# Two graph layers on one core: block turns on VectorE and an exchange through DRAM in place of TensorE transposes

## The chip, the cores and the metric

The kernel runs on one core of one Trainium2 chip. Each of the core's engines has its own queue of instructions: TensorE (PE; its weight loads are listed as PEld), VectorE (DVE), ScalarE (ACT), GpSimd (POOL) and SyncE (SP), which here only issues DMAs. POOL issues DMAs too. The metric is device time in microseconds (us), the median of several runs. Durations of instructions come from one further execution, which the hardware profiler recorded.

## The reference

There are 16 graphs (batches) of 1024 nodes with 128 features, and an adjacency matrix of zeros and ones for each. Two residual blocks follow one another.

```python
h = relu(layernorm(x))                       # block 0
for i in range(4):                           # gated layers, GRU cell
    m = einsum('bjn,bjd->bnd', adj, h @ weight[i])
    r = sigmoid(xr + hr); z = sigmoid(xz + hz); n = tanh(xn + r * hn)
    h = (1 - z) * n + z * h                  # xr, xz, xn from m @ w_ih[i].T, hr, hz, hn from h @ w_hh[i].T
x = x + h * nodemask[:, :, None]
h = relu(layernorm(x))                       # block 1
for i in range(4):                           # graph convolution
    h = relu(einsum('bnm,bmc->bnc', adj, h @ W[i]) + b[i])
    h = gamma[i] * (h - mean) * rsqrt(var + 1e-5) + beta[i]   # mean and var over all batches and nodes
x = x + h
```

## The kernel before

`exact_path` does the work. (A flag, found by looking at the low bits of every adjacency value, would choose the slower `general_path` for other data; it isn't taken here.) All values are f32; a matmul with the adjacency takes the features as the sum of two f32r tiles, a rounded part and a rest (`hw[0]` and `hw[1]`, 128 nodes by 128 features for each block), so that the sum is as good as f32.

**The first stage** (to about 1240 us) is block 0. The weight of a layer is folded into the input weights of the gates (`w_mT`), so h itself is aggregated. The gates want h with the features on the partitions (128 x 1024, two halves of 512 nodes), the aggregation wants it as weights with the nodes on the partitions. So h is turned in each layer: `features_times` with `w` None (L491) makes eight 128x128 transposes on TensorE (L498), ScalarE copies the rounded part out of PSUM (L502), VectorE subtracts the rest (L503). `turn` (L639, L647) brings the normalized y of a new batch into the layout of the gates; `tail_norm` (L651, L657) turns the last h back, adds it to x with the mask (L660), takes the sums of the next layer norm, and stores the result (`xmid_d`, and its normalized form, `ymid_d`).

Two streams, A for the even batches (`sa`) and B for the odd ones (`sb`), take turns. `half_step(one, two)` (L856) does the gates of `two` (`gate_step`, L781, once for each half: twelve f32 matmuls in pairs, sigmoid, two VectorE operations, tanh, sigmoid, three VectorE operations) and the aggregation of `one` (`agg_step`, 32 matmuls of 128x512, L525, then ScalarE copies of the result m, L770, that the next half-step's gates take). Before them it splits `one`'s h (L859). A layer of both streams is two half-steps, a pair of batches eight. Beside this run:

- `finish` (L829): when a batch has gone through its four layers, `tail_norm`, and `take` (L736), which loads the eight row tiles of 512 KB of the stream's next batch (`load_rows`, L577, on SP) into the slots of the old ones. A stream aggregates a new batch's layer 0 in the half-step that follows.
- `copy_rows` (L572): the next adjacency is copied from the input into a DRAM scratch (`raw`), 8 DMAs of 512 KB on POOL; the loads take it from there.
- `transpose_rows` (L591): GpSimd casts a row tile to bf16, SP issues a DMA transpose into `adjT`, which POOL stores (`adjT_d`, 2 MB) for the second stage. One tile `adjT` serves both streams, two tiles `half1` hold the casts.
- `ahead` (L817): loads x of the next batch (POOL), normalizes it, turns it. `look_on` (L838): four `look`s (L589) at a time, a maximum over the low bits of a row tile on VectorE.

In the start-up (L880) the order of all engines is that of the code. In the steady loop (L995 to L1004) this holds for POOL and SP alone; on PE, DVE and ACT a planner orders what is ready by its own costs, with a few edges by `behind` (L683). POOL and SP work strictly in order: an instruction that waits holds up everything behind it.

**The second stage** is block 1: the stored turned adjacency is loaded (`load_adjT`, L1018), widened to f32r, and aggregated; the last part adds x and stores the output.

Of the kernel before, what the change touches and what calls it, by code (L numbers as in the profile page):

```python
# [8 lines left out]
F32 = mybir.dt.float32  # L9
# [332 lines left out]
def exact_path(  # L342
# [57 lines left out]

    def hw_tiles(b, name):
        return [keep.tile([P, N], F32R, tag=f"hw{b % 2}{s}", name=f"{name}_{s}") for s in range(2)]
# [14 lines left out]
    maskT = const.tile([P, B * NB], F32, tag="maskT", name="maskT")  # L417
    NV = 2 * 3 * L + 3 * L
# [27 lines left out]
    def turn_small(vn, mn):  # L446
# [6 lines left out]
        nc.vector.tensor_copy(maskT, pt[:, : B * NB])  # L453

# [79 lines left out]
    with ExitStack() as st:  # L534
# [3 lines left out]
        def load_x(b, eng):  # L538
            xt = flat(f"x{b}")
            eng.dma_start(xt, x[b].rearrange("(k p) c -> p k c", p=P))  # L540
            return xt

        raws = {}
# [28 lines left out]
        def copy_rows(b):  # L572
            raws[b] = rawd.tile([N, N], F32, tag="raw", name=f"raw{b}")
            for j in range(NB):
                nc.gpsimd.dma_start(raws[b][j * P : (j + 1) * P, :], adj[b][j * P : (j + 1) * P, :])
# [15 lines left out]
        def transpose_rows(b, row, j, adjT):  # L591

            t = work.tile([P, N], BF16, tag="half1", name=f"half{b}_{j}", bufs=2)
            nc.gpsimd.tensor_copy(t, row.bitcast(F32))  # L594
            nc.sync.dma_start_transpose(adjT[:, :, j * P : (j + 1) * P], t)

        def norm(xt, y, name):

            norm_apply(xt, y, norm_stats(xt, name))
# [39 lines left out]
        def turn(y, name, hT=None, func=AF.Copy):  # L639

            if hT is None:
                hT = work.tile([P, N], F32, tag="h", name=f"h_{name}", bufs=7)
# [8 lines left out]
        def tail_norm(b, xt, hT):  # L651

            for hf in range(NH):
                pt = tmp(f"pt_x{b}_{hf}")
                for q in range(BH):
                    k = hf * BH + q
                    nc.tensor.transpose(pt[:, q * P : (q + 1) * P], hT[:, k * P : (k + 1) * P], ident)  # L657
                for q in range(BH):
                    k = hf * BH + q
                    nc.vector.scalar_tensor_tensor(  # L660
                        xt[:, k, :],
                        pt[:, q * P : (q + 1) * P],
                        maskT[:, b * NB + k : b * NB + k + 1],
                        xt[:, k, :],
                        ALU.mult,
                        ALU.add,
                    )
# [5 lines left out]
            nc.gpsimd.dma_start(xmid_d[b].rearrange("(k p) c -> p k c", p=P), xt)  # L673

            def rest():
                norm_apply(xt, y, nt)
# [4 lines left out]
        written = [True]  # L681

        def behind(*inss):  # L683

            es = ExitStack()
            for ins in () if written[0] else inss:
                es.enter_context(tc.issue_after(ins.ins))
            return es

        class Stream:  # L690


            def __init__(self, first):
                self.b, self.i, self.rest, self.tag = first, 0, None, "AB"[first % 2]
                self.opened = None
# [31 lines left out]
            def prepare(self, b, xt):  # L727
                y = work.tile([P, N], F32, tag=f"y{self.tag}", name=f"y_in{b}", bufs=1)
                norm(xt, y, f"in{b}")
                self.ready = b, xt, y  # L730

            def prepare_turn(self):
                b, xt, y = self.ready
                self.ready = xt, y, turn(y, f"in{b}")
# [6 lines left out]
            def split_step(self):  # L741
                nm = f"{self.b}_{self.i}"
                self.hw = hw_tiles(self.b, f"ghw{nm}")
                for g in range(NH):
                    if self.i > 0:
                        features_times(None, self.hT, self.hw, g, f"g{nm}")
                        continue
                    self.split_high(g)
                    self.split_low(g)

# [30 lines left out]
            def gate_step(self, hf, between=None):  # L781
# [30 lines left out]
                self.last_dve = nc.vector.tensor_add(ho, ho, r)  # L812
                if hf == NH - 1:
                    self.hT = self.new
                    self.i += 1

            def ahead(self):  # L817

# [477 lines left out]
```

## Time and profile before

| | |
|---|---|
| median of 3 runs | 1840.94 us (1840.56 to 1841.36) |
| the profiled execution | 1840.61 us, of which the span from its first to its last instruction is 1838.8 us |
| busy, share of the span | PE 99%, PEld 68%, DVE 67%, ACT 56%, POOL 15% |
| granted TensorE clock | 0.999 |
| DMA | 381 MB, mean 207 GB/s |
| row loads, `row<-raw` | 112 of 512 KB, 5.8 us from issue to landing in the median |
| copies of the adjacency, `raw<-in_adj_dram` | 112 of 512 KB, 11.6 us |

Busy times count an instruction from its start to its end, and matmuls overlap; so durations of PE are read from the distance of starts. A table of instructions in time gives start, duration, engine, line, operation, output and inputs, and in brackets how long the engine was idle before and what ended that.

### The profile page before, as it was taken

The page shows a single profiled execution, that of the slowest core. Times are in us where ns is not written, and L with a number is a line of the kernel's source. Part 1 is how long each engine was busy: PE and PEld are TensorE (multiplying, and loading weights), DVE is VectorE, ACT ScalarE, POOL GpSimd, SP SyncE. Part 2 cuts the span into 40 slices and gives each one's busy share as a digit, 9 for nine tenths or more (in the row PEclk, how much of TensorE's full clock was granted, in tenths as well). Part 3 has the DMA queues.
Part 4 walks back from the last instruction along what each step waited for, and adds up shares of the span by engine and source line. Part 5 has one row for each costly group of instructions (what it writes and reads, how often), then busy time and mean ns, then how long its engine had stood idle before and what let it go on. Part 6 is the DMA issues. An engine that isn't in the chain of part 4 may idle for free.

```text
span 1838.8 us, 21960 instructions
## 1 busy us (share of the span) xinstructions
PE 1821.5 (99%) x7326; PEld 1254.2 (68%) x7326; DVE 1225.6 (67%) x2244; ACT 1035.8 (56%) x1577; POOL 285.0 (15%) x378
## 2 busy tenths in 40 slices
PE   9999999999999999999999999999999999999997
PEld 6566666656566666666565666667778888888886
DVE  7656667567666766766766757676666666666665
ACT  5544454553545554445355353467777767767764
POOL 4131320230231042023023013011100000000011
PEclk9999999999999999999999999999999999999999
DMA  7189775575486386567557546349876676767676
GB/s 264 39 247 317 209 229 195 162 206 192 159 233 180 126 233 178 196 172 217 218 159 206 178 145 172 103 159 332 291 248 228 212 256 204 257 209 260 210 249 242
DMA packets 256280, 381.21 MB, mean 207 GB/s; under 512 B 149932, under 2 KB 155856, under 8 KB 252320
## 3 DMA queue, kind: packets, MB, share of 16 engines
q1 hardware_dynamic: 237968, 245.95, 44.2%
q0 software_dynamic: 17664, 133.53, 20.4%
q8 instruction: 59, 0.97, 0.2%
q14 instruction: 61, 0.50, 0.1%
q10 hardware_dynamic: 528, 0.26, 0.0%
HBM read 287.39 MB, written 117.44 MB: 220 GB/s over the span
## 4 chain that ended last, share of the span: by engine, by line
PE 94%; DVE 2%; ACT 2%; issue 1%; DMA 1%; SPq 0%; POOL 0%; DVEq 0%; ACTq 0%; POOLq 0%
PE pm L525 24%; PE pc_m L525 12%; PE g_r L790 11%; PE g_z L790 11%; PE pc_g_r L525 6%; PE pc_g_z L525 6%; PE g_hn L790 6%; PE g_xn L790 6%; PE hw_c L500 4%; PE hw_g L498 2%; PE pw_g_hn L1096 1%; PE pw_g_xn L1096 1%; PE pt_in L647 1%; PE pt_x L657 1%; PE pc_g_r L510 1%
## 5 line engine op out<-in xcount | busy, mean ns | idle before, releaser
L525 PE MATMUL pm<-row,ghw 128*128 128x512 f32 x2048 | 515.6, 406 | 0.1
L525 PEld LDWEIGHTS pm<-row,ghw 128*128 128x128 f32 x2048 | 383.2, 188 | 112.6 <-issue 36.9
L525 PE MATMUL pc_m<-wide,chw 128*128 128x512 f32 x1024 | 246.0, 395 | 0.0
L525 PEld LDWEIGHTS pc_m<-wide,chw 128*128 128x128 f32 x1024 | 190.5, 188 | 42.3 <-issue 4.3
L807 ACT ACTIVATE r<-r,vecs 128x512 f32<-128x512 f32 x128 | 92.3, 721 | 216.8 <-DVE r L804 216.8
L525 PE MATMUL pc_g_r<-wide,chw 128*128 128x512 f32 x464 | 187.0, 403 | 0.3 <-ACT chw L502 0.3
L525 PE MATMUL pc_g_z<-wide,chw 128*128 128x512 f32 x464 | 180.9, 390 | 0.0
L594 POOL CAST half<-row 128x1024 bf16<-128x1024 f32 x128 | 139.7, 1108 | 250.9 <-DMA adjT<-half 169.6
L1028 DVE CAST wide<-packed 128x1024 fp32r<-128x1024 bf16 x160 | 110.0, 692 | 74.5 <-PE pc_m L525 56.4
L1028 DVE CAST wide<-block 128x1024 fp32r<-128x1024 bf16 x160 | 110.2, 691 | 73.2 <-PE pc_g_z L525 40.2
L503 DVE TENSOR_TENSOR ghw<-hw_g,ghw 128x512 fp32r<-128x512 f32 x96 | 62.0, 686 | 129.7 <-ACT ghw L502 129.5
L1026 ACT CAST wide<-block 128x1024 fp32r<-128x1024 bf16 x96 | 100.6, 1048 | 59.3 <-PE pc_m L525 34.3
L803 DVE SCALAR_TENSOR_TENSOR r<-g_hn,vecs,r 128x512 f32<-128x512 f32 x128 | 95.4, 745 | 56.8 <-ACT r L802 31.3
L1026 ACT CAST wide<-packed 128x1024 fp32r<-128x1024 bf16 x96 | 100.7, 1049 | 55.6 <-PE pc_g_z L525 23.7
L790 PE MATMUL g_r<-m,w_mT 128*128 128x512 f32 x256 | 130.7, 592 | 0.0
L790 PE MATMUL g_z<-m,w_mT 128*128 128x512 f32 x256 | 130.7, 592 | 0.0
L790 PE MATMUL g_xn<-m,w_mT 128*128 128x512 f32 x256 | 130.7, 592 | 0.0
L589 DVE TENSOR_REDUCE low<-row 128x1 f32<-128x1024 uint16 x112 | 128.6, 1210 | 0.0
L808 ACT ACTIVATE z<-g_z,brz 128x512 f32<-128x512 f32 x128 | 87.1, 680 | 71.0 <-PE g_z L790 71.0
L770 ACT COPY m<-pm 128x512 f32<-128x512 f32 x128 | 68.8, 586 | 101.3 <-PE pm L525 101.2
L802 ACT ACTIVATE r<-g_r,brz 128x512 f32<-128x512 f32 x128 | 87.7, 685 | 60.3 <-PE g_r L790 59.5
L810 DVE TENSOR_TENSOR h<-h,r 128x512 f32<-128x512 f32 x96 | 74.6, 777 | 62.4 <-ACT r L807 62.4
(176 smaller groups left out, 2764.0 us busy)
## 6 DMA issues: line engine op xcount, KB each, us to landing
packed<-adjT_d SPq DMA_DIRECT2D x256, 256.0 KB, 5.9
block<-adjT_d SPq DMA_DIRECT2D x256, 256.0 KB, 5.4
raw<-in_adj_dram POOLq DMA_DIRECT2D x112, 512.0 KB, 11.6
row<-raw SPq DMA_DIRECT2D x112, 512.0 KB, 5.8
adjT_d<-adjT POOLq DMA_DIRECT2D x16, 2048.0 KB, 7.9
xmid_d<-x POOLq DMA_DIRECT2D x16, 512.0 KB, 4.8
y<-ymid_d POOLq DMA_DIRECT2D x16, 512.0 KB, 5.1
ymid_d<-y_mid POOLq DMA_DIRECT2D x15, 512.0 KB, 3.0
```

The costliest lines, as they stand in the source:

```text
L500: nc.tensor.matmul(pt[:, q * P : (q + 1) * P], src, w, start=True, stop=True)
L525: nc.tensor.matmul(pm[hf], hw[s][:, j * P : (j + 1) * P], rows[j][:, hf * HALF : (hf + 1) * HALF], start=(j == 0 and s == 0), stop=(j == N ...
L589: nc.vector.tensor_reduce(low[:, k : k + 1], lows, axis=AX.X, op=ALU.max)
L594: nc.gpsimd.tensor_copy(t, row.bitcast(F32))
L790: nc.tensor.matmul(po, wT[:, i, g * C : (g + 1) * C], rhs, start=start, stop=stop)
L802: nc.scalar.activation(r, pr, AF.Sigmoid, bias=brz[:, 3 * i : 3 * i + 1])
L803: nc.vector.scalar_tensor_tensor(r, phn, b_hn(i), r, ALU.add, ALU.mult)
L807: nc.scalar.activation(r, r, AF.Tanh, bias=b_in(i))
L808: self.last_act = nc.scalar.activation(z, pz, AF.Sigmoid, bias=brz[:, 3 * i + 1 : 3 * i + 2])
L810: nc.vector.tensor_sub(ho, hin, r)
L1026: nc.scalar.copy(r, t)
L1028: nc.vector.tensor_copy(r, t)
```

## The change

Batches 0 and 1 (`plain`) are done as before. For the others the transposes of h and y no longer run on TensorE. VectorE turns a half (128 x 512) in blocks of 32x32, which leaves each block in the right orientation and in the wrong group of 32 partitions. The half is then written to a DRAM scratch (`cross`, 256 KB) and read back by four DMAs, one for each group of 32 partitions, which pick its blocks from all four groups. All these DMAs are issued on SP.

```diff
+        def exchange_out(t, name):
+            d = rawd.tile([P, HALF], F32, tag="cross", name=f"cross_{name}", bufs=6)
+            nc.sync.dma_start(d, t)
+            return d
+
+        def exchange_in(d, t):
+            src = d.rearrange("(t r) (s x) -> s r t x", t=4, s=4)
+            for s in range(4):
+                nc.sync.dma_start(t[s * 32 : (s + 1) * 32, :].rearrange("r (t x) -> r t x", t=4), src[s])
...
+        def turn_across(y, name):
+            hT = work.tile([P, N], F32, tag="h", name=f"h_{name}", bufs=7)
+            for hf in range(NH):
+                cols = slice(hf * HALF, (hf + 1) * HALF)
+                t = half_tile(f"ty_{name}_{hf}").bitcast(F32)
+                nc.vector.transpose(t, y[:, cols].rearrange("p (k a c) -> p a k c", a=4, c=32))
+                exchange_in(exchange_out(t, f"{name}_{hf}"), hT[:, cols])
+            return hT
```

The gates end with the turn and the way out, and the way back follows: the first half's at once, the second half's (`two.exchange()`) in `half_step`. In the next half-step, between the gates' operations of the other stream, ScalarE and VectorE split the returned tile (`split_part`), which they read in runs of 32 columns.

```diff
             def gate_step(self, hf, between=None):
...
+                else:
+                    nc.vector.tensor_add(ho, ho, r)
+                    if not plain(self.b):
+                        t = half_tile(f"th{nm}").bitcast(F32)
+                        nc.vector.transpose(t, ho)
+                        self.outs[hf] = exchange_out(t, f"h{nm}")
+                if hf == 0:
+                    self.exchange()
...
+        def turn_rows():
+            for b, row, j in waiting_rows[:2]:
+                if j == 0:
+                    adjTs[b] = turned_tile(f"adjT{b}")
+                transpose_rows(b, row, j, adjTs[b])
+                if j == NB - 1:
+                    nc.gpsimd.dma_start(adjT_d[b], adjTs[b])
+            del waiting_rows[:2]
+            for dst, src in copies[:2]:
+                nc.gpsimd.dma_start(dst, src)
+            del copies[:2]
+
+        def beside_aggregation(one, two):
+            if one.b + 2 < B and one.i == 2:
+                one.next_apply()
+            if two.ends:
+                two.ends.pop(0)()
+            if one.ends:
+                one.ends.pop(0)()
+            if two.b + 2 < B and two.i == 2:
+                two.next_sums()
+            if one.b + 2 < B and one.i == 3:
+                one.next_turn()
+            one.look_on()
+
         def half_step(one, two, gated=None, halfway=None):
-            if one.i > 0:
+            if one.i == 1:
+                one.give_rows()
+            by_turns = plain(one.b) and one.i > 0
+            if by_turns:
                 one.split_step()
-            two.gate_step(0)
-            two.gate_step(1)
+            for hf in range(NH):
+                two.gate_step(hf, None if by_turns else lambda: one.split_part(hf))
             if gated:
                 gated()
-            if one.i == 0:
-                one.split_step()
+            turn_rows()
+            two.exchange()
+            if two.i == 1:
+                two.ahead()
+            turn_rows()
+            beside_aggregation(one, two)
             one.agg_step(0)
             if halfway:
                 halfway()
-            if one.rest:
-                with behind(two.last_act):
-                    one.rest()
-                one.rest = None
-            two.ahead()
-            one.look_on(two)
             one.agg_step(1)
             two.finish()
```

`next_sums`, `next_apply` and `next_turn` are the former normalization and turn of the next batch's y, the last now with `turn_across` in layer 3. `tail_norm` of the batches 2 to 13 reads the exchanged tile in place of a turn on TensorE, one half-step later than before; the batches 14 and 15 keep their last turn on TensorE. The copies of the adjacency and its row transposes, eight of each at once before, come as two and two in each half-step.

The block turns put the nodes of a half in another order (node 128q+32k+i at place 128k+32q+i). So for these batches x and the adjacency's rows are copied to DRAM in that order (`order_x`, and the two patterns in `copy_rows`), the cast of a row tile reorders its columns, the mask has a second map (`maskB`), `xmid` is brought back by a DRAM copy, and the ReLU of the last convolution writes its columns in the reference's order.

The steady loop's order is that of the code on every engine:

```diff
-        with tc.manual_schedule(engines={mybir.EngineType.Pool, mybir.EngineType.SP}):
-            written[0] = False
+            turn_mask(load_mask())
+        with tc.manual_schedule(engines=every):
             for s in range(2, B // 2 * L):
                 half_step(sa, sb)
                 half_step(sb, sa)
```

In the second stage two kinds of buffers change places (`load_adjT`, `fetch_x`).

## The prediction

> **What bounds the kernel now.** I read the busy shares first, then the chain, then PE's, VectorE's and SP's instructions in time over one pair of batches (563.5 to 713.5 us), then the table of stretches. The page:
>
> ```profile
> PE 1821.5 (99%) x7326; PEld 1254.2 (68%) x7326; DVE 1225.6 (67%) x2244; ACT 1035.8 (56%) x1577; POOL 285.0 (15%) x378
> ...
> PE 94%; DVE 2%; ACT 2%; issue 1%; DMA 1%; SPq 0%; POOL 0%; DVEq 0%; ACTq 0%; POOLq 0%
> ```
>
> TensorE is busy all the time and the chain is TensorE's. PE in time, one half-step (gates of one stream, aggregation of the other) and what surrounds it:
>
> ```profile
> 589.97 1.04 PE L498 MATMUL hw_g<-ident,h 128*128 128x128 f32 x8
> 590.84 1.02 PE L790 MATMUL g_r<-h,w_hhT 128*128 128x512 f32 x2
> ...
> 595.99 1.02 PE L790 MATMUL g_r<-h,w_hhT 128*128 128x512 f32 x2
> ...
> 600.74 7.85 PE L525 MATMUL pm<-row,ghw 128*128 128x512 f32 x32
> 608.42 1.03 PE L657 MATMUL pt_x<-ident,h 128*128 128x128 f32 x8
> 609.29 1.02 PE L790 MATMUL g_r<-h,w_hhT 128*128 128x512 f32 x2
> ```
>
> Read the starts, since matmuls overlap: eight turns take 590.84-589.97 = 0.87 us, one half of the gates 595.99-590.84 = 5.15, so both 10.30, and the aggregation 608.42-590.84-10.30 = 7.28. A half-step is 18.45 us, with no gap. Eight of them and two more groups of eight turns (L647) make 149.3, and the stretch says:
>
> ```profile
> 563.50:713.50 150.00, 150.00 (x530) 92.64 (x529) 102.69 (x202) 74.66 (x128) 31.32 (x41) 1.00 0.61 190
> ```
>
> Columns: stretch, then PE, PEld, DVE, ACT, POOL, granted clock, share of the 16 DMA engines, GB/s. What leaves PE here is time won, until another thing is late. The second stage (from about 1240 us) keeps its work.
>
> **What goes.** For each batch from 2 on: turns of h in layers 1 to 3 (3 x 8), of y (8), and for batches 2 to 13 of the last h (8). That is 14 x 4 + 12 = 68 groups of eight, 68 x 0.87 = **59 us**: 52 in the six pairs 2/3 to 12/13, 5 in the last pair, 2 in the first. A half-step of a middle pair becomes 17.58.
>
> **What VectorE and ScalarE get.** Neither the 32x32 turn nor a strided read of a turned tile is in this trace. The nearest row for the turn is a 128x512 f32 operation on VectorE:
>
> ```profile
> 593.69 0.75 DVE L803 SCALAR_TENSOR_TENSOR r<-g_hn,vecs,r 128x512 f32<-128x512 f32 x1
> ...
> 597.70 0.69 DVE L812 TENSOR_TENSOR h<-h,r 128x512 f32<-128x512 f32 x1
> 598.84 0.75 DVE L803 SCALAR_TENSOR_TENSOR r<-g_hn,vecs,r 128x512 f32<-128x512 f32 x1 [0.45 <-PE g_hn L790]
> ```
>
> I take 0.69; the bounds are 0.26 (a 128x128 pass, L609) and 1.21 (the 128x1024 16-bit pass, L589). The turned h lies 597.70+0.72+0.69-590.84 = 8.3 us into the half-step for the first half. The second half starts behind it and is turned at 13.7 (4.0 from its first operation to its last add, 0.72, 0.69). The split's subtraction (0.69) fits the 0.79 in which VectorE waited for the tanh, and ScalarE's copy (0.6) fits its 1.8 us wait for VectorE. Beside the aggregation come at most 4.7 (four looks of 1.21 pipelined, or multiply-adds and sums, 609.48 to 614.4) and two more turns (1.3). So VectorE ends at 18.4 to 19.7, and is wanted again at 17.58+2.85 = 20.4. It fits with 1 us to spare. At 1.21 per turn it would be over by about 1 us in some half-steps: +0 to 15 in all. ScalarE: root, table load and eight ReLUs follow VectorE's second half and end at 17.6 as the m copies become due. I put 0; at 0.3 each time it is 8.
>
> **What SP's queue gets; here I see the loss.** Each exchange is one issue out, a wait until it has landed, and four issues in; all stand on SP in written order, in front of whatever comes later, the row loads of the stream's next batch included. Issue is 0.32 us (L581). SP's stores of 128 and 256 KB landed in 2.1 at best (L1243; medians of 2.4 to 4.7 in its groups); I take 2.3. One exchange holds SP for 2.3+0.1+4x0.32 = **3.7 us**; bounds 3.3 and 4.4. Half-step (B, layer 3) has four in a row: two of A's last h, two of B's next y. SP starts the second at 13.7, so it is free at 13.7+3x3.7 = 24.8, which is 7.2 us into the next half-step. Only then come A's eight row loads. Now they come early:
>
> ```profile
> 582.90 7.58 SPq L581 DMA_DIRECT2D row<-raw  x8
> ```
>
> That is 17.8 us before the aggregation of 600.74 uses them. Afterwards PE wants the first row 10.3 us in, one more each 0.91, and is done at 17.58. The first lands 3.2 after its issue at best (L581), the others 1.55 apart (512 KB at the 339 GB/s of 603 to 613):
>
> ```profile
> 603.00:613.00 10.00, 10.00 (x42) 7.02 (x41) 9.18 (x25) 2.79 (x5) 0.92 (x1) 1.00 0.96 339
> ```
>
> Row 7 lands at 7.2+3.2+7x1.55 = 21.3, and its four matmuls end at 22.3: **PE waits 5 us** (3.4 and 7.4 at the bounds). Next, B's last two exchanges are queued behind these loads: out at 22.8, SP through with both at 22.8+1.3+3.7 = 27.8, B's loads start 5.4 into the following half-step of which they are wanted 10.3 in; row 7 lands at 19.5: **3 us** more (2 to 5). Then A's exchanged h of that half-step waits behind B's loads, comes some 4 us late to the split, and moves tanh, the z that frees a bank, and the m copies: **2 us** (0 to 5). So 10 us at a change of batch.
>
> How often? The change from the first pair has no exchange of h (batches 0 and 1 are turned on TensorE): two exchanges end 3.4 us into the half-step and cost nothing. The six later ones cost 6 x 10 = **60 us** (35 to 100).
>
> **DMA and POOL in the middle half-steps.** Today's share is 0.61 of 150 = 92 us a pair. Twenty exchanges of 2 x 256 KB and 2 MB of reordered x and xmid are 12.6 MB, 37 us at 339 GB/s; together 129 of about 141. The row turns of one stream wait on SP for the other's adjT store (7.9 to landing) in front of an exchange; its half arrives 1 to 2 us late, most of it absorbed (PE wants the split only 14 us in). I put 1.5 a pair, 9 in all (0 to 30). The mask's turn, two maps of x and the reordered copies are small or long before use: 0 (0 to 8). Stage two's strided ReLU: 0; covered by aggregation.
>
> The Trainium skill, "DMA: Bandwidth & Descriptors", rules for kernel authors, speaks against splitting: transfers to disjoint partitions share the same engines, one 128-partition transfer is better, and under 64 KB one mostly pays overhead; the four parts of each return are 64 KB. The same page's fit, about 2.0 us + bytes / 436 GB/s, gives an estimate of 2.6 us for the store where the trace has 2.1 at best; by 2.6 an exchange holds SP 4.0 us and the row wait is about 1 us longer per change of batch.
>
> **Sum.** The profiled execution took 1840.61 us (span 1838.8 and 1.8 around it); the median of the runs is 1840.94, so the two can be read as one. 1840.6 - 59 + 60 + 9 = **1850**. The signs depend on sizes that nearly cancel, and I say so.
>
> **Rivals.**
> - *The loads arrive in time* (faster). If SP is through earlier, because stores to DRAM land faster than 2.1 us for a lone transfer or the loads of 4 MB find idle engines, the waits shrink to about 2 us a pair: 1840.6 - 59 + 12 = 1794. For it: PE wants rows one after another, and between 573 and 583 the DMA share is 0.19. Against it: every issue-to-landing in the trace is above 2 us, and four lie in a row. It decides if a boundary costs under 9 us.
> - *DMA becomes the bound* (slower). A 512 KB store in 512-byte pieces (xmid, 4.8 us) lands 1.8 us later than one in 4 KB pieces (ymid, 3.0). If the returns cost 0.9 each by that, 20 x 0.9 = 18 us come on top of 129: 147 of DMA in a pair of 141, unevenly spread (raw copies landed in 11.6). Six pairs of 147 + 10 instead of 150 are +42, less 7 in the others: about 1876; with VectorE's lateness 1890. For it: today's share already reaches 1.05 in places. Against: most of the load is not urgent.
> - *Written order itself costs* where the planner filled gaps: some 15 us on top of the forecast, 1865; or the turns are only replaced without effect on the cadence, no change.
>
> **Chances.** Forecast (boundary waits of 6 to 15 us) 0.50: 0.07 of it faster, 0.09 the same, 0.34 slower. Loads in time 0.27, faster. DMA bound 0.20, slower. The last 0.03: 0.01 faster, 0.02 slower. A measurement of this kernel can tell about 0.2% (3.7 us) from no change. Faster 0.35, same 0.09, slower 0.56. For the range I take 1790 (most of the case of loads in time) to 1895 (most of the DMA case); the likeliest case alone is 1825 to 1880.
>
> **What would show it.** Right: no L498, pt_in or pt_x groups for later batches; PE steps of 17.6 us inside a pair; PE idle in front of L525 released by a DMA of row<-raw, at each change of batch from batch 2 on, with the row loads issued only some 7 us into the half-step; SP's own waits led by its exchange stores. Wrong: PE near 99% busy (loads in time); a DMA share near 1 through whole pairs with waits everywhere (DMA bound); idle PE in front of the gates, released by ScalarE's m (written order); turns far from 0.69 us.

## The result and the profile after

The changed kernel takes **2070.6 us** (median; 2068.1 to 2078.9) beside 1841.2 for the kernel before: ratio 1.125, interval 1.122 to 1.129. The prediction was 1850, with a range of 1790 to 1895. The side was right, the size was not: the loss is 230 us where 9 were forecast.

All of it lies in the first stage. The first instruction of the second stage's sums (pt_deg) starts at 1228.5 us in the profile before and at 1456.6 after; the rest of the program keeps its length. The page after, busy shares and chain:

```profile
PE 1837.3 (89%) x6786; PEld 1213.6 (59%) x6786; DVE 1318.2 (64%) x2381; ACT 1023.2 (49%) x1549; POOL 349.7 (17%) x548
...
PE 43%; DMA 30%; DVE 11%; ACT 6%; SPq 5%; issue 4%; POOL 1%; DVEq 0%; ACTq 0%; POOLq 0%
```

TensorE runs 540 instructions fewer and yet is "busy" 16 us longer than before. Its share of the chain falls from 94% to 43%, and 30% are now transfers, which had 1%. VectorE, which got the turns, stands at 64%: it isn't the bound.

TensorE in time at a change of batch (start, duration, instruction, idle time before it in brackets):

```profile
354.40 1.02 PE L865 MATMUL g_r<-h,w_hhT 128*128 128x512 f32 x2
...
363.84 1.02 PE L865 MATMUL g_z<-m,w_mT 128*128 128x512 f32 x2
374.23 3.78 PE L558 MATMUL pm<-row,ghw 128*128 128x512 f32 x8 [9.36 <-DMA row<-raw]
...
386.47 1.02 PE L865 MATMUL g_r<-h_in,w_hhT 128*128 128x512 f32 x2
```

The gates of both halves end as before, then TensorE stands still for 9.36 us until the first row has landed. The half-step lasts 32.1 us (386.47-354.40) instead of 17.58. The eight matmuls behind the pause take 3.78 us, 0.47 each; in the profile before, 32 of them take 7.28, 0.23 each. The clock was down as well.

SP's queue over the same time shows why the rows are late:

```profile
333.47 1.25 SPq L628 DMA_DIRECT2D cross_h<-th  x1
343.64 2.05 SPq L635 DMA_DIRECT2D nh<-cross_h  x4
345.79 0.38 SPq L628 DMA_DIRECT2D cross_in<-ty_in  x1
348.04 1.73 SPq L635 DMA_DIRECT2D h_in<-cross_in  x4
...
369.73 4.78 SPq L641 DMA_DIRECT2D row<-raw  x8
374.60 0.57 SPq L628 DMA_DIRECT2D cross_h<-th  x1
386.11 1.75 SPq L635 DMA_DIRECT2D nh<-cross_h  x4
```

An undisturbed exchange is a store, 2.2 us until its loads can be issued, and 1.73 for those: 4.1 us, as from 345.79 to 349.87. But the store of 333.47 lets its loads go only at 343.64, and that of 374.60, right behind eight row loads, at 386.11. GpSimd's queue just ahead of the first of these:

```profile
330.87 0.55 POOL L958 DMA_DIRECT2D adjT_d<-adjT  x1 [3.92 <-DMA adjT<-half]
331.41 1.09 POOL L961 DMA_DIRECT2D raw<-in_adj_dram  x2
```

These are 2 MB of turned rows and two copies of 512 KB. The exchange came while they were on their way. SP then runs one exchange after another and reaches the row loads 15.3 us into the half-step (369.73-354.40). It is the same at all six changes of batch: some 20 us before the change a store comes 2.5 to 5.6 us behind 2 MB and two copies, its loads can go 7.8 to 10.2 us after it, and the row loads are reached 13.4 to 17.7 us into the half-step.

In the middle half-steps a late return costs in another way. In the one that starts at 657.66 (ScalarE, then TensorE):

```profile
669.35 0.62 ACT L823 CAST ghw<-nh 128x512 fp32r<-128x512 f32 x1 [7.97 <-DMA nh<-cross_h]
...
670.49 0.67 ACT L883 ACTIVATE z<-g_z,brz 128x512 f32<-128x512 f32 x1
```
```profile
671.21 1.67 PE L865 MATMUL g_z<-h,w_hhT 128*128 128x512 f32 x2 [4.27 <-ACT z L883]
```

ScalarE's copy of the returned half stands in the written order ahead of its tanh and its z, and TensorE's next g_z, which could have followed at 666.8, waits for that z. Here the store had landed in 4.0 us; the four loads, issued beside 2 MB of turned rows and four copies, took 8.7 to 9.9. In the whole run TensorE waits 70.4 us for z and 70.8 for rows.

The second place is the start, which the prediction had put at nothing:

```profile
124.59 0.63 PE L485 MATMUL pt_mb<-ident,mb 32*128 32x32 f32 x4 [40.19 <-POOL mb L478]
```

Four small turns of the mask wait 40.2 us for GpSimd. In its order the reordering of the mask (L478) stands behind a load of x that itself waited 35.1 us for the buffer of w_g (until 83 us), and then behind row casts that wait for row turns, copies, and the mask's own load, which it waits 7.0 us for.

**Where the time stands.** I measured every half-step from 294 to 1426 us by the starts of its gates and took off 17.58. The six changes of batch cost 86 us in their first half-step (11 to 17 each), 19 in the second and 34 in the third: 138. The other 33 half-steps cost 97 together. Of these, TensorE waits 64 for rows in the first half-steps and 8 in the second, 22 for z in the third, and 48 for z and 20 for m in the other 33; the rest is slower work. With 40 at the mask and -59 for the turns, 1840.6 becomes 2057; about 14 us are left for the first pair and the passage to the second stage.

**A part of it is clock.** One pair of batches after, and the same work in a run without the exchange (e2, below); columns: stretch, length, busy time of PE, PEld, DVE, ACT and POOL with their instructions, granted clock, DMA share, GB/s:

```profile
538.13:722.01 183.88, 154.46 (x449) 88.61 (x448) 116.65 (x222) 72.52 (x125) 40.36 (x64) 0.92 0.74 226
```
```profile
433.39:574.03 140.64, 140.64 (x449) 84.45 (x448) 116.51 (x220) 73.78 (x126) 47.16 (x73) 1.00 0.80 229
```

The same 449 instructions on TensorE take 13.8 us more, so of 43 us in a pair 29 are idle and 14 are slower work. The stretches of this pair in which the granted clock was 0.50 hold 20.0 us of that work, 10 more than at 1.00: the clock is a quarter of the 43. The other 4 go with the 15 pauses; I take them for lost overlap (a pair of gate matmuls lasts 1.02 us, but the next one starts 0.86 after it), which no run shows apart. The granted clock is 0.50 from 374 to 378, behind the pause of 9.36 us, and 1.00 from 378.2 on. After idle 4.41 us two gate matmuls take 2.07 (420.39), after 1.71 us 1.13 (345.30), with 1.02 as usual. The Trainium skill, "TensorE: Matmul & The Clock Gate", section "What's actually happening", says that an idle window of about 3.4 us halves the clock until the array has been busy as long. These pauses agree with it.

### The profile page after: what moved, and what is told of

It reads as the page before. It is cut to its first block, busy times and chain, and to the rows that moved or that the text cites. A ratio compares the mean times of both kernels' runs of the same rounds, so it can differ in the third digit from the quotient of the medians.

```text
span 2068.5 us, 22404 instructions
## 1 busy us (share of the span) xinstructions
PE 1837.3 (89%) x6786; PEld 1213.6 (59%) x6786; DVE 1318.2 (64%) x2381; ACT 1023.2 (49%) x1549; POOL 349.7 (17%) x548
## 4 chain that ended last, share of the span: by engine, by line
PE 43%; DMA 30%; DVE 11%; ACT 6%; SPq 5%; issue 4%; POOL 1%; DVEq 0%; ACTq 0%; POOLq 0%
PE pc_m L558 11%; DMA cross_h<-th 9%; DMA nh<-cross_h 9%; PE pm L558 5%; DMA row<-raw 5%; PE pc_g_r L558 5%; PE pc_g_z L558 5%; PE hw_c L533 4%; PE g_r L865 3%; PE g_z L865 3%; SPq L635 3%; DMA adjT<-half 3%; DVE h L886 2%; PE g_hn L865 2%; DVE low L649 1%
## 5 line engine op out<-in xcount | busy, mean ns | idle before, releaser
L558 PE MATMUL pm<-row,ghw 128*128 128x512 f32 x2048 | 546.5, 420 | 73.2 <-DMA row<-raw 70.8
L558 PEld LDWEIGHTS pm<-row,ghw 128*128 128x128 f32 x2048 | 394.1, 196 | 220.4 <-DMA row<-raw 101.4
L558 PE MATMUL pc_m<-wide,chw 128*128 128x512 f32 x1024 | 245.5, 395 | 1.8 <-ACT chw L1215 1.3
L558 PEld LDWEIGHTS pc_m<-wide,chw 128*128 128x128 f32 x1024 | 190.3, 188 | 44.3 <-issue 3.8
L659 POOL CAST half<-row 128x512 bf16<-128x512 f32 x224 | 147.2, 697 | 289.3 <-DMA adjT<-half 192.4
L558 PE MATMUL pc_g_r<-wide,chw 128*128 128x512 f32 x464 | 186.8, 403 | 0.3 <-ACT chw L535 0.3
L558 PE MATMUL pc_g_z<-wide,chw 128*128 128x512 f32 x464 | 180.9, 390 | 0.0
L823 ACT CAST ghw<-nh 128x512 fp32r<-128x512 f32 x84 | 51.8, 617 | 254.3 <-DMA nh<-cross_h 254.3
L824 DVE TENSOR_TENSOR ghw<-nh,ghw 128x512 fp32r<-128x512 f32 x84 | 58.7, 698 | 153.0 <-ACT ghw L823 153.0
L865 PE MATMUL g_z<-h,w_hhT 128*128 128x512 f32 x192 | 103.7, 623 | 47.8 <-ACT z L883 47.8
L865 PE MATMUL g_z<-m,w_mT 128*128 128x512 f32 x256 | 140.1, 631 | 0.0
```

The costliest lines, as they stand in the source:

```text
L558: nc.tensor.matmul(pm[hf], hw[s][:, j * P : (j + 1) * P], rows[j][:, hf * HALF : (hf + 1) * HALF], start=(j == 0 and s == 0), stop=(j == N ...
L659: nc.gpsimd.tensor_copy(by_blocks(t[:, cols]), by_columns(row.bitcast(F32)[:, cols]))
L865: nc.tensor.matmul(po, wT[:, i, g * C : (g + 1) * C], rhs, start=start, stop=stop)
```

## Theories

*Theory 1*: the order on SP. Every exchange holds SP for its round trip, and the row loads stand behind four of them. *Theory 1b* (formed after e3): a queue delivers in order, so a store behind row loads waits for them. *Theory 2*: the bulk transfers (GpSimd's copies, the 2 MB stores, the rows) fill the DMA engines, and whatever store comes meanwhile lands late. *Rival*: the written order of all engines, or VectorE's turns, cost by themselves.

## Experiments

Ratios are to the kernel before, with their interval. Diffs are against the changed kernel unless a run is named.

**e1: the mask turned later.**
```diff
-            turn_mask(load_mask())
...
             for s in range(2, B // 2 * L):
                 half_step(sa, sb)
+                if s == 2:
+                    mb = load_mask()
                 half_step(sb, sa)
+                if s == 3:
+                    turn_mask(mb)
```


> The mask's load, its reordering by GpSimd and its turn on TensorE stand later in the written order: load behind the first half-step of the third round (layer 2 of batches 0 and 1), turn two half-steps later, both before batch 2 first needs it. Theory (the turn stood where GpSimd was still waiting for x's buffer, so TensorE lay idle 40.2 us in front of L485): that idle time goes and nothing else waits in its place, 2070 - 40 = 2030 us (2020 to 2040). Rival (GpSimd's work of that time is late for something else too, the row turns and the raw copies): the wait moves to another instruction and at most 15 us are won, 2055 us or more.

2038 us (1.107, 1.104 to 1.110), 32 less. The turn now waits 0.9 us; some 8 of the 40 come back in one half-step of the first pair (27.8 us, 20.3 before this edit). The mask is one cause, and e8 shows that it is a separate one.

**e2: no exchange.**
```diff
-                        self.outs[hf] = exchange_out(t, f"h{nm}")
+                        self.outs[hf] = t
...
-                    exchange_in(self.outs[hf], t)
-                    self.parts.append(t)
+                    self.parts.append(self.outs[hf])
```
(and y turned straight into hT)


> Leaves out the exchange of partition groups through DRAM, stores and loads both: the tiles that VectorE turned in 32x32 blocks are used as they are. The VectorE turns, the written order of all engines, the reordered copies and the mask stay. Theory 1 and 2 together (the exchange is the loss, by SP's order or by its transfers): about 1841 - 59 + 40 (mask) + 0 to 15 = 1820 to 1840 us, and TensorE waits for rows no more. Rival (the written order of all engines or the turns on VectorE cost, exchange or not): half-steps stay over 19 us, 1950 us or more.

1870 us (1.015, 1.013 to 1.018), 201 less and 30 above what was expected. Nearly every half-step from 220 us to the end of the first stage is 17.58 long, with TensorE busy throughout (the second of the two stretches above). So the rival falls: neither the written order nor VectorE's turns cost anything in the steady part. The turns themselves, 711 ns for h and 672 for y on average here as in the changed kernel, are what had been reckoned. The changed kernel's line for h:

```profile
L897 DVE STREAM_TRANSPOSE th<-h 128x512 f32<-128x512 f32 x108 | 76.8, 711 | 3.7
```

The 30 us above the upper end are a pause of 30.3 at the passage to the second stage (pc_m, released by VectorE's cast of "wide"): the last row turns were late there, since GpSimd had waited 57.6 us at a load of the second stage placed ahead of them.

**e3: the row loads a half-step earlier.**
```diff
+            if two.i == L - 1 and two.b + 2 < B:
+                two.next_rows = load_rows(two.b + 2)
...
-                self.rows = load_rows(self.b)
+                self.rows = self.next_rows
```


> The eight row loads of a stream's next batch are issued one half-step earlier: at the start of the half-step of its last gates, in front of that half-step's exchanges on SP, not behind them. Theory 1 (place on SP): the waits for rows at the change of batch go, 7 to 16 us in the first half-step and 2 to 4 in the second, six times: about -100, 1970 us (1950 to 1990). Theory 2 (transfers in flight stretch each other): the 4 MB now run beside the exchanges of that half-step, whose stores take 10 us and more, and the exchanged h is late instead: at most -50, 2020 us or more.

2066 us (1.122, 1.113 to 1.131): no gain clear of the noise. The wait for rows did shrink (idle before L558 73.2 to 25.9 us in all), but the exchanged halves came late instead. SP in that run:

```profile
381.28 5.41 SPq L641 DMA_DIRECT2D row<-raw  x8
386.79 0.77 SPq L628 DMA_DIRECT2D cross_h<-th  x1
396.94 1.74 SPq L635 DMA_DIRECT2D nh<-cross_h  x4
```

The loads of the store right behind the rows go out 10.2 us after it, those of the next one (399.08) 2.2 after it. The rows' place on SP alone is not the cause.

**e4: both stores ahead of the loads.**
```diff
-                if hf == 0:
-                    self.exchange()
-                else:
+                if hf == NH - 1:
+                    self.exchange()
                     self.hT = self.new
```
(and in turn_across both exchange_out before both exchange_in)


> Both stores of a pair of exchanges are issued before the first of its loads (h of both halves, and y of both halves), so that SP waits about once per pair of round trips, not twice. Nothing else moves. Theory 1 (SP is held by one round trip after another): each pair frees SP some 3 to 5 us earlier, at the changes of batch four of them in a row; -40 us, 2030 us (2010 to 2045). Theory 2 (the landing is slow because other transfers are in flight, and the first half's return, which is needed first, now stands behind the second store): within 15 us of 2070.

1988 us (1.080, 1.077 to 1.083), 82 less, twice what Theory 1 had said. SP's own waits (what it waited for, us in total, times, longest), after and in e4:

```profile
SPq L635 <- DMA cross_h<-th: 417.9, 87, 15.2
```
```profile
SPq L635 <- DMA cross_h<-th: 136.9, 31, 10.2
```

The stores land no sooner (median 5.2 in both); SP only waits once for two. So the round trips one after another are a cause. Their size goes with the landings: the 87 waits were 4.8 us each on average, where an undisturbed store asks for 2.2. By the starts of the gates, 59 of the 82 us are won at the changes of batch (138 falls to 79) and 13 in the middle half-steps.

**e5: few copies.**
```diff
-                if self.b + 2 < B:
+                if self.b < 2:
                     copies.extend(copy_rows(self.b + 2))
+                elif self.b + 2 < B:
+                    raws[self.b + 2] = raws[self.b]
```


> Leaves out GpSimd's reordered copies of the adjacency from batch 4 on (batches 2 and 3 are read again in their place): 10 x 4 MB read and written again, some 84 of 467 MB. SP's order is untouched. Theory 2 (the exchange's stores land late because GpSimd's copies fill the DMA engines): the stores' median falls from 5.2 toward 2.5 us and the half-steps of layers 1 to 3 shrink; -60 us or more, 2010 us or less. Theory 1b (a store lands late because row loads and row turns stand ahead of it on the same SP queue, which delivers in order; copies run on another queue): at most -20, 2050 us or more.

1967 us (1.068, 1.065 to 1.071), 104 less. The kernel leaves out 96 of the 112 copies (twelve batches, not ten), 50 MB of the 467 as the page counts them. The stores' median falls as Theory 2 says (after, then e5):

```profile
cross_h<-th SPq DMA_DIRECT2D x108, 256.0 KB, 5.2
```
```profile
cross_h<-th SPq DMA_DIRECT2D x108, 256.0 KB, 2.3
```

The middle half-steps come down to between 17.6 and 23.4, mostly under 20. The changes of batch stay at 25 to 28, 19 to 23 and 18 to 24: there eight row loads stand ahead of a store, and no run takes these away. By the starts of the gates, 57 of the 104 us are won in the middle half-steps (97 falls to 40) and 43 at the changes (138 to 95).

**e6: row loads on ScalarE's queue.**
```diff
-                nc.sync.dma_start(t.bitcast(F32), raws[b]...
+                nc.scalar.dma_start(t.bitcast(F32), raws[b]...
```


> The eight row loads at a change of batch are issued by ScalarE, on its own DMA queue, at the same place in the half-step as before; SP keeps exchanges and row turns. Theory 1b (in the run with the row loads moved ahead, a store right behind eight row loads landed in 9.6 us and the next in 1.8: a queue delivers in order): rows no longer wait for four exchanges and stores no longer stand behind rows; the half-steps at the change fall from 32 to about 20 and from 21 to 18 us and the next ones lose their lateness: -100 us, 1970 us (1940 to 1990). Theory 2 (the 16 engines are shared whatever the queue): the rows come early but the stores beside them still take some 10 us, as with the rows moved ahead: 2040 us or more.

2079 us (1.129, 1.126 to 1.132): no gain, and Theory 1b's 1970 is far off. TensorE waits only 1.4 us for rows in all, but ScalarE is held (ScalarE's queue; the issues of eight row loads in ns, shortest, median and longest; SP's queue):

```profile
365.81 14.96 ACTq L641 DMA_DIRECT2D row<-raw  x7
380.82 0.69 ACT L877 ACTIVATE r<-g_r,brz 128x512 f32<-128x512 f32 x1 [14.72 <-DMA row<-raw]
```
```profile
L641 ACTq DMA_DIRECT2D row<-raw x8: 326/342/368, 365.3 to 380.4; - x8
```
```profile
366.83 0.38 SPq L628 DMA_DIRECT2D cross_h<-th  x1
372.19 1.83 SPq L635 DMA_DIRECT2D nh<-cross_h  x4
```

Seven row loads keep ScalarE for 15 us, in which it can't compute: the gates of the next half-step wait 11 to 15 us for its r at the six changes of batch. The issues themselves take 0.34 us each. Between them ScalarE waits, before five of the seven until a transfer of SP's has landed whose completion semaphore the row load takes over: the one of 369.47 goes when the exchange's load of 365.36 has landed at 369.38.

Stores on SP still wait 5.4 and 6.3 us (366.83 and 374.12) beside rows on another queue, so a common queue is not the whole cause. But their median falls:

```profile
cross_h<-th SPq DMA_DIRECT2D x108, 256.0 KB, 3.2
```

And in the changed kernel the store of 374.60 lands at 386.04, 0.65 us after the last of the eight rows ahead of it on SP. So Theory 1b may hold for a part, behind row loads; as ScalarE's waits cost time of their own, this run doesn't settle it. The Trainium skill, "DMA: Bandwidth & Descriptors", section "Issuing engines are not separate DMA queues", says that all issuers end on the same 16 engines, and that issuing elsewhere saves issue time only, usually small. The late stores beside ScalarE's rows agree with the first, and 0.34 us an issue with the second.

**e7: e1, e4 and e6 together.**


> Three edits together: the mask turned later, both stores of a pair ahead of its loads, the row loads on ScalarE's queue. If the causes are separate, their gains add: 2070 - 32 - 82 - what the row loads on ScalarE bring alone (100 by theory 1b, 20 by theory 2), so 1860 by theory 1b and 1935 by theory 2. If the stores ahead and the row loads remove the same wait, 30 to 50 us more than that sum.

2010 us (1.092, 1.089 to 1.095), slower than either view allowed. ScalarE's waits remain (g_r waits 10 to 12 us for its r at every change of batch).

**e8: e1 and e4 together.**


> The mask turned later and both stores of a pair ahead of its loads, together; the row loads stay on SP. If the two causes are separate, 2070 - 32 - 82 = 1956 us (1945 to 1965). If the run with three edits was slow because the two edits hinder each other (and not because ScalarE was held 15 us by the issue of eight row loads), about 2000 us.

1952 us (1.060, 1.055 to 1.065), 118 less: the two add.

**e9: e8, and the row turns last.**
```diff
-            turn_rows()
             two.exchange()
+            turn_rows()
             if two.i == 1:
                 two.ahead()
             turn_rows()
```


> The run with two edits, and on SP the loads of the second half's exchange ahead of the half-step's row turns (and on GpSimd nothing else moved than by that). Theory (the second half's return stands behind two row turns that wait for GpSimd's casts; seen on SP as two turns of 4 to 7 us in all between the two groups of four loads, in four half-steps of a stream's eight): some 3 us in 24 half-steps, a half of it felt by TensorE: -35 us, 1920 us (1905 to 1940). Rival (SP has spare time there, the return is late by its store's landing): within 10 us of the run with two edits.

2008 us (1.090, 1.077 to 1.103): 55 worse than e8, a miss for both views. SP:

```profile
566.08 15.35 SPq L660 DMA_TRANSPOSE adjT<-half  x4
581.52 1.10 SPq L628 DMA_DIRECT2D cross_h<-th  x2
599.14 4.04 SPq L635 DMA_DIRECT2D nh<-cross_h  x8
```

Four row turns in a row wait for GpSimd's casts, which have two buffers between them, and hold SP for 15 us; the next half-step's stores then come at 581.5 and land behind GpSimd's copies at 599.

**e10: e9, with only h of layers 1 to 3 exchanged.** y and the last h are turned on TensorE again.
```diff
-                t = half_tile(f"ty_{name}_{hf}").bitcast(F32)
-                nc.vector.transpose(t, ...)
-                exchange_in(exchange_out(t, f"{name}_{hf}"), hT[:, cols])
+                for q in range(BH):
+                    nc.tensor.transpose(pt[...], y[...], ident)
+                nc.scalar.copy(by_columns(hT[:, cols]), by_blocks(pt))
...
-                return self.b >= B - 2 and self.i == L - 1
+                return not plain(self.b) and self.i == L - 1
```


> The run with the row turns last, with only h of layers 1 to 3 exchanged: y of the next batch and the last h are turned on TensorE again, as in the kernel before (26 groups of eight, 23 us given back). SP then has no exchange in the half-steps where a stream changes its batch. Theory 1 (four exchanges in a row ahead of the row loads, and their round trips beside 8 MB of rows): H of the change falls from 24 to 19 us and the two behind it by 2 to 5; +23 - 6 x 12 = -50 us against the run with the row turns last. Theory 2 alone (bulk copies in the middle half-steps): +10 to +25 us against it, since only the turns come back.

1900 us (1.031, 1.028 to 1.034), 108 below e9. Theory 1 had -50, Theory 2 had +10 to +25: the cause is Theory 1's, at twice its size. The changes of batch now take 18.5, 17.6 and 18.8 us. Slow half-steps are left only where row turns and copies are under way (21 to 24, 19 to 22, 21 to 26).

**e11: e9 with few copies.**


> The run with the row turns last, and GpSimd's reordered copies of the adjacency left out from batch 4 on. Theory 2 (the copies' transfers are what remains in the middle half-steps): these fall to 17.6 to 18.5 us, only the changes of batch stay at 24 and 20; 1841 - 59 + 6 x 12 + some 25 at the passage to the second stage, about 1870 us (1850 to 1890). Theory 1 (SP's order is what remains): less than 25 us under the run with the row turns last.

1937 us (1.052, 1.049 to 1.055), 71 below e9 and 67 above Theory 2's number: the row turns last (e9) are in it too.

**e12: e10 without e9's edit.**


> As the run with only h of layers 1 to 3 exchanged, but the row turns stand between the two groups of loads again, as in the change itself (mask late and stores first stay). Theory (four row turns in a row hold SP for 8 to 15 us, since two buffers make each wait for GpSimd, and the next half-step's store waits behind them; putting them last cost 55 us in the run without this edit): the three slow half-steps of a pair (23, 19.5 and 22 us) fall by some 2 us each, 1900 - 6 x 6 = 1865 us (1845 to 1875). Rival (without exchanges of y and of the last h there is room on SP): 1890 to 1905, no difference.

1871.1 us (1.016, 1.014 to 1.018), 28 below e10 and inside the theory's range. Against e8 it is 81 us faster, though the turns on TensorE give 23 back: the exchanges of y and of the last h had cost some 104.

**e13: e8 with few copies.**


> The run with two edits (1952 us), and the reordered copies of the adjacency left out from batch 4 on. Theory 2 (in the middle half-steps the exchange's stores are late by the copies' transfers alone): the 104 us that leaving them out was worth in the change itself shrink, since the stores ahead have already won part of it: 1870 to 1890 us, with middle half-steps of 17.6 to 18.5 and changes of batch of 24 and 20. Theory 1 (the row turns and the order on SP): 1920 us or more.

1890 us (1.027, 1.025 to 1.029), 62 below e8: less than e5's 104. SP waits for 21 stores of h here and for 80 in e5.

**e14: e12 with few copies.**


> The run with only h of layers 1 to 3 exchanged and the row turns between, and the reordered copies left out from batch 4 on: no exchange at the change of batch, no bulk copies in the middle. If the named causes are all (the mask, round trips one after another, copies in flight, four exchanges ahead of the row loads), every half-step is 17.6 to 18.5 us, and the time is 1841 - 36 (42 groups of eight turns) + 10 (first pair) + 10 to 30 (passage to the second stage) = 1825 to 1845 us. If half-steps over 20 us remain, there is a cause that I haven't named.

1823.6 us (0.991, 0.989 to 0.993). No half-step after the first pair is over 19.4, and TensorE is the bound again:

```profile
PE 1789.2 (98%) x6994; PEld 1220.5 (67%) x6994; DVE 1288.3 (71%) x2329; ACT 1035.4 (57%) x1577; POOL 295.5 (16%) x452
...
cross_h<-th SPq DMA_DIRECT2D x84, 256.0 KB, 2.1
```

By this run's own test, no cause without a name is left. The steps on the way are 118 (mask, round trips), 81 (exchanges at the change of batch, with 23 given back) and 47.5 (copies in flight). That they lead from 2070.6 to 1824 proves nothing, since each is the difference from the run before, and what a cause is worth depends on the order: the copies were worth 104 in e5, 62 in e13 and 47.5 here.

**e15: e12 with the copies spread over all eight half-steps of a pair; e16: with them at the end of each half-step.**
```diff
-            if one.i == 1:
-                one.give_rows()
+            if one.i == (1 if plain(one.b) else 0):
+                one.give_copies()
+            if one.i == 1:
+                one.give_rows()
...
-            for dst, src in copies[:2]:
+            n = 1 if 4 in raws else 2
+            for dst, src in copies[:n]:
...
```
(`give_copies` is the part of `give_rows` that lists the copies; e16: the loop, with twice n, behind agg_step(1))


> The run with h of layers 1 to 3 alone exchanged, the row turns between (1871 us): its reordered copies of the adjacency start one layer earlier and are issued two a half-step through all eight half-steps of a pair, not four a half-step through four. All work is done. Theory 2 (48 us of that run, 1871 - 1824, are copies in flight beside an exchange's store, four and a 2 MB store at a time): with half as many in flight at a time a store is late by some 3 us less, which the slack of the exchange mostly takes up: 1871 - 25 = 1846 us (1835 to 1855), beside 1841 before. Rival (the delay goes with the amount copied, not with how much is in flight at once, so the same wait is only spread): 1863 us or more.

> As the run with spread copies, but both copies of a half-step stand at its end in GpSimd's order, behind the row turns, instead of one behind each pair of row turns. Theory 2: 1 MB that starts at the end of a half-step is through (3 us at 339 GB/s) before the next half-step's first store at 8 us: 1835 us (1825 to 1845), faster than spread by 5 to 15. Rival (GpSimd reaches its instructions late, since its casts wait for the row turns on SP, so the place in its order says little about the time): the same as spread within 5 us.

e15: 1854.5 us (1.006, 1.004 to 1.008); e16: 1858.9 (1.010, 1.008 to 1.011). Spreading wins 17 of the 47.5, at the upper end of Theory 2's range. The place in GpSimd's order says little, as the rival of e16 had it: GpSimd reaches it late. In e15:

```profile
737.79 0.55 POOL L956 DMA_DIRECT2D adjT_d<-adjT  x1 [3.66 <-DMA adjT<-half]
738.33 2.69 POOL L960 DMA_DIRECT2D raw<-in_adj_dram  x5
```
```profile
735.48 4.47 SPq L628 DMA_DIRECT2D cross_h<-th  x2
740.05 10.20 SPq L635 DMA_DIRECT2D nh<-cross_h  x8
```

GpSimd had waited for the row turns and issues five copies at once behind the 2 MB store, just as an exchange is on its way.

**e17: e15 with the row turns a layer earlier.**
```diff
             if one.i == (1 if plain(one.b) else 0):
                 one.give_copies()
-            if one.i == 1:
-                one.give_rows()
+                one.give_rows()
```


> The run with spread copies (1855 us), and each batch's row turns begin one layer earlier too, in the half-step that has no exchange on SP (its rows have just landed there), so that they and the 2 MB store of the turned rows are out of the half-steps of layers 2 and 3, where SP now reaches an exchange's store late and finds that store and up to five copies in flight. All work is done. Theory (what remains is the meeting of row turns, that store and copies with the exchanges, some 10 us a pair in three half-steps): half of it goes, 1855 - 6 x 5 = 1825 to 1842 us, equal to the kernel before or just under it. Rival (the rows land late in the half-step in which they are turned, GpSimd's order is held there, and the next half-step's exchange waits instead): 1850 us or more.

1962 us (1.067, 1.065 to 1.068): slower as the rival said and by more, though not for its reason. GpSimd:

```profile
672.12 0.92 POOL L744 DMA_DIRECT2D xm_d<-x  x1 [61.75 <-DVE st_mid L670]
673.03 2.27 POOL L659 CAST half<-row 128x512 bf16<-128x512 f32 x4
```

In its order the store of xm, which waits for the tail's sums on VectorE, stands ahead of the casts, so SP's row turns wait for both, and the exchanges behind them. It is that store that holds GpSimd for 61.8 us, not rows that land late.

No version that does all the work is faster than the kernel before; e15 comes within 0.6%. A kernel without the copies that still reads every batch in its own order wasn't tried.

## Why the prediction was wrong, step by step

- **What goes (59 us, half-step 17.58): right.** e2 has a pair of 140.64 us, eight times 17.58.
- **What VectorE and ScalarE get (turn 0.69, cost 0): right.** The turn is 0.71 and 0.67, and e2's steps stay at 17.58. The written order, too, costs nothing in the steady part.
- **SP's queue (60 us): right in place, wrong in size; here lies the step that failed.** A lone exchange holds SP 4.1 us (3.7 forecast), the row loads do stand behind a line of them, B's half-step costs 3.2 us more on average (3 forecast), and the exchange right behind eight row loads takes 11.5 us (the forecast has it issued at 7.2+8x0.32 = 9.8 and landed at 22.8, 13 us). What failed is the landing of a store at "2.1 at best", taken as 2.3 for every exchange but that one. The median is 5.2, and some 20 us before each change of batch one store meets GpSimd's 2 MB and two copies, so that its loads go 8 to 10 us after it. SP starts the line of four late and its row loads go out 13 to 18 us into the half-step, not 7.2. The waits became 14.3 + 3.2 + 5.6 a change, where 5 + 3 + 2 were forecast: 138 us instead of 60. The trace before had warned: medians up to 4.7 for such stores, and 11.6 for the copies.
- **DMA and POOL in the middle half-steps (9, at most 30): wrong, 97.** A half was to be 1 to 2 us late, and "most of it absorbed (PE wants the split only 14 us in)". A quarter of the stores of h landed after 9 us or more, against 2.1 alone, and ScalarE's copy of the first half has to be done before its tanh and z, which TensorE's second g_z waits for: in the half-step of 657.66 the half was wanted some 7 us in (g_z at 9.1, less 1.9 for copy, tanh and z), not 14. e5 takes most copies away and wins 57 of the 97.
- **The mask (0 to 8): wrong, 32** by e1. I asked whether the mask was long before use, and not where its turn stood in two written orders. TensorE has to pass the turn, whoever needs its result, and GpSimd comes to the mask late.
- **Not priced at all: the clock.** Pauses were counted at their length. The work between and after them takes about 14 us a pair more, of which 10 are the clock's.
- **The rival "DMA becomes the bound"** was nearest in mechanism. DMA engines are busy 136 us in a pair (0.74 of 183.88), where I had 129 and the rival 147. It failed by its price (1876 to 1890) and by its sign, a DMA share near 1 through whole pairs: a pair's total against its length says how full the engines are, but not how late a single transfer lands among the others.
- **Open:** how much of a store's lateness behind row loads is SP's queue and how much is the engines that all queues share.

## What to carry to other kernels

A round trip through DRAM inside a tight cadence is to be priced at what its transfer takes amid the bulk that will be in flight, not at the best row of the trace: here 2 us alone and 10 behind 3 to 4 MB. What counts as its deadline is the first instruction in any written order that takes the result: here ScalarE's copy some 7 us into the half-step, not the aggregation. List, for each instruction that is put into a written order, what stands ahead of it on the engine that produces its operand: a mask behind a waiting load, casts and copies in GpSimd's order made TensorE wait 40 us, and moving row turns on SP or GpSimd twice made things worse (55 and 108 us). A small gain on the bound engine (0.87 us here) is lost as soon as what replaces it is late by more.

## What was not expected of the hardware

- Moving loads to another engine's queue can hold that engine, though an issue is short: in e6 the issues took 0.33 to 0.37 us, but seven of them kept ScalarE for 15.0 us, since five waited for transfers of SP's queue to land.
- With the rows on ScalarE's queue the stores on SP shown above still waited 5.4 and 6.3 us, against 2.2 undisturbed; their median was 3.2, against 5.2 with the rows on SP.
- TensorE's granted clock was 0.50 for about 4 us behind a pause of 9.36 us, and a pause of 4.41 us doubled the gate matmuls behind it, while 1.71 us did not.
